# Moving two small normalisation products, one drain and one projection copy within a causal attention kernel

## The chip, the cores and the metric

The kernel runs on one core of one Trainium2 chip. The metric is device time in microseconds (us) for the whole program, from its first to its last instruction; the figure given is the median of three runs. Everything is 32-bit float. The names of the engines are those of the profile: PE for matrix products and PEld for their weight loads, ACT for ScalarE, DVE for VectorE, POOL for GpSimd, and SP for the engine whose queue here only issues transfers.

## The reference

The input `x` is 32 images of 256 channels by 32 by 32, that is 32 batches of 256 channels by 1024 positions. Group normalisation is followed by strictly causal attention of 8 heads with 32 channels each, and the result is added to `x`:

```python
g = gn(x)                                   # 32 groups of 8 channels, over channels and positions
q  = q_w  @ g + q_b                         # 256 x 1024
kv = kv_w @ g + kv_b                        # k, v: 256 x 1024 each
scores = (q^T k) / sqrt(32)                 # per head; a position sees only earlier ones
attn = softmax(scores), 0 where masked      # position 0 sees none and gets 0
return x + attn @ v
```

## The kernel before

**Visits.** A batch is worked off in N = 12 *visits*, six for each half of the heads (`g` = 0, 1). The list `visits` (L506 to L517) says which two pieces of the transposed score matrix a visit computes: one "full" piece of 512 columns by 128 keys for four heads, and one "half" piece of 256 columns. The main loop (L606 to L615) writes every engine's queue by hand, visit by visit over all 32 x 12 visits, and engines follow this order strictly. In visit `i` the loop puts down

1. `scores(i)` (L301): PE computes the two pieces into three PSUM tiles of two banks (tag `sT`, three buffers, so each visit uses all three); ACT takes three exponentials of 1024 columns each, two of the full piece (L326, into `e`) and one of the half piece (L327, into `eh`); POOL masks the diagonal (L294) where the piece has one;
2. what is filed under `at[i]`: most often one projection of the next or the same batch, 16 or 32 products into a PSUM bank and one ACT copy out of it (`project_qk`, L221, or `project_v`, L237), and issues of transfers by SP;
3. `values(i - 1)` (L338): PE multiplies the exponentials of the visit before with `v` into the bank `acc`; DVE adds the exponentials up (L354) for the softmax's denominator; at the end of a half row ACT copies `acc` to `num` (L357);
4. what is filed under `after[i]`: steps of the normalisation, folds of the sums, finishing steps.

Visits are counted below from 0 to 11 within a batch; "the fourth visit" is number 3.

**One spare bank.** [...] six hold the scores, one is `acc`, and the last has the tag `misc` with one buffer (L129, L132). Through it go, one after the other, the projection of each visit, the two products of the normalisation (`pm` in `norm_mean`, L184, and `pv` in `norm_variance`, L201) and the denominators of a whole batch (`pd` in `sum_folded`, L373). Each of these must wait until ACT has copied the one before it out of the bank. (In the first batch a few projections use `acc` instead, L159.)

**Projections.** The twelve projections of a batch are placed at visits -5 to 6 (`PROJECT`, L538), so one falls into each visit: visits 7 to 11 serve the next batch, visits 0 to 6 the present one. The last, in visit 6, is `k` of the second half of the heads.

**Normalisation** of batch b (`prepare`, L524) has eight steps filed under `after`, placed by `PREPARE` (L539) relative to the batch's first visit: DVE statistics of the two channel halves (-18, -17), the product `pm` with its ACT copy (-16, that is visit 8 two batches ahead), the deviation on DVE (-15), the product `pv` with its ACT copy (-14), the power on POOL (L209, at -12) and the two halves of the normalised `xn` on DVE (L216, both at -11, which is visit 1). The first two batches are placed separately.

**Denominators.** For each batch but the last two, POOL issues two adding transfers for each of the four half rows (`fold`, L363): partitions 64 to 127 onto 0 to 63 after visit `SUMS[n]` = 3, 7, 9, 13 and 32 to 63 onto 0 to 31 two visits later. The second waits for the landing of the first, and both stand in POOL's queue with the masks. Two more visits later SP brings the 32 rows into `folded` (`stack`, L367). In visit 18, which is visit 6 of the next batch, PE sums them (`pd`), ACT copies the result, and SP sends it through DRAM; DVE inverts it (L439), and `finish` (L453, DVE) writes the output after visits 12, 12, 13 and 14 of the next batch. SP also loads `x` two batches ahead, in visit 3 (`load`, L115), behind the output stores of visits 0 to 2.

**`shifted`** (L625) is a second, safe program under a condition that is false for these inputs; only it reads `v_bias` (L683), which is loaded at the start (L143).

Of the kernel before, what the change touches and what calls it, by code (L numbers as in the profile page):

```python
# [9 lines left out]
F32 = mybir.dt.float32  # L10
I32 = mybir.dt.int32
AF = mybir.ActivationFunctionType
# [5 lines left out]
P = 128  # L18
HD = 32
# [12 lines left out]
def tile_norm_attention_residual(  # L32
# [19 lines left out]
    nc = tc.nc  # L52
    B, C, H, W = x.shape
# [51 lines left out]
    wT = const.tile([P, NG, 3 * C], F32, name="wT")  # L105
    qk_bias = const.tile([P, 2, NG], F32, name="qk_bias")
    v_bias_col = const.tile([P, NG], F32, name="v_bias_col")
    v_bias = const.tile([P, C], F32, name="v_bias")

    def unshifted():  # L110
        live = {}
# [24 lines left out]
        def load_weights():  # L136
            for n, w in enumerate((q_w, kv_w[0:C], kv_w[C : 2 * C])):
                live["wn", n] = epool.tile([P, 4, HALFBANK], F32, tag="eh", bufs=4, name=f"wn_{n}")[:, :NG, :C]
                nc.scalar.dma_start(out=live["wn", n], in_=w.rearrange("(o p) c -> p o c", p=P))
            nc.scalar.dma_start(out=qk_bias[:, 0, :], in_=q_b.rearrange("(g p) -> p g", p=P))  # L140
            nc.scalar.dma_start(out=qk_bias[:, 1, :], in_=kv_b[0:C].rearrange("(g p) -> p g", p=P))
            nc.scalar.dma_start(out=v_bias_col, in_=kv_b[C : 2 * C].rearrange("(g p) -> p g", p=P))
            nc.scalar.dma_start(out=v_bias, in_=kv_b[C : 2 * C].rearrange("(o c) -> o c", o=1).broadcast_to([P, C]))  # L143

        def turn_weights(n):
            wn = live["wn", n]
# [151 lines left out]
            if k == 0:  # L298
                nc.gpsimd.memset(e[0:1, :, 0:1], 1.0)

        def scores(b, full, half):  # L301


            tag = "e0" if full[2] == 0 else "e"
            name = f"{b}_{full[0]}_{full[1]}_{full[2]}"
            e = epool.tile([P, 4, HALF], F32, tag=tag, bufs=4 if tag == "e0" else 3, name=f"{tag}_{name}")
            eh = epool.tile([P, 4, HALFBANK], F32, tag="eh", bufs=4, name=f"eh_{name}")
            pairs = [ps_s.tile([P, 2, HALF], F32, tag="sT", name=f"sT_{name}_{a}") for a in range(3)]
            short = pairs[2].rearrange("p bank (n q) -> p bank n q", n=2)
            first = [scores_of((b, half), short[:, j % 2, 1, :], j) for j in (2, 3)]  # L310
            for j in range(4):
                scores_of((b, full), pairs[j // 2][:, j % 2, :], j)

            for ins in first:
                ins.then_inc(bank_free, 1)
                tc.no_tile_sem_insts.add(ins.ins.name)
            live["free"] = live.get("free", 0) + len(first)
            wait = nc.tensor.wait_ge(bank_free, live["free"])
            for ins in first:
                tc.declare_no_dep(wait.ins, ins.ins, reason="the semaphore orders them")  # L320
            for j in range(2):
                lo = scores_of((b, half), short[:, j, 0, :], j)
                for ins in first:
                    tc.declare_no_dep(lo.ins, ins.ins, reason="the semaphore orders them")
            for a in range(2):
                nc.scalar.activation(e[:, 2 * a : 2 * a + 2, :], pairs[a], AF.Exp)  # L326
            exp = nc.scalar.activation(eh.rearrange("p (n bank) q -> p bank n q", n=2), short, AF.Exp)  # L327

            for ins in first:
                tc.add_to_no_dep_group(f"first_{name}", ins.ins)  # L330
                tc.add_to_no_dep_group("first", ins.ins)
            tc.declare_no_dep(exp.ins, group=f"first_{name}", reason="through the last two products")
            tc.declare_fence(exp.ins, group=f"first_{name}")
            mask(full, e)
            mask(half, eh)
            live["e", b, full], live["e", b, half] = e, eh
# [25 lines left out]

        def fold(b, n, rows):  # L363
            total = live["sum", b, *divmod(n, NH)]
            nc.gpsimd.dma_start(out=total[:rows], in_=total[rows : 2 * rows], accum_op=ALU.add)  # L365

        def stack(b, n):  # L367
# [168 lines left out]


        PROJECT = (-5, -4, -3, -2, -1, 0, 1, 2, 3, 4, 5, 6)  # L538
        PREPARE = (-18, -17, -16, -15, -14, -12, -11, -11)  # L539
        SUMS = (3, 7, 9, 13)  # L540

        FINISH = ((N + 12, N + 12, N + 13, N + 14), (N + 7, N + 7, N + 8, N + 9))
# [1 line left out]

        with tc.manual_schedule(engines={ENG.PE, ENG.Activation, ENG.DVE, ENG.Pool}):
            load_weights()
            turn_weights(0)
            for g in range(NG):
                norm_channels(0, g)
            keep_busy(2)  # L550
            norm_mean(0)
            turn_weights(1)
            norm_deviation(0)
            norm_variance(0)
            norm_rstd(0)
            turn_weights(2)
            keep_busy(4)
            for hf in range(NH):
                norm_apply(0, slice(hf * HALF, (hf + 1) * HALF))
            nc.vector.tensor_scalar_mul(qk_bias[:, 0, :], qk_bias[:, 0, :], SCALE)  # L560
            units = projections(0)
            for n, f in zip((None, None, 0, 0, 0, 0) + PROJECT[6:], units):
                if n is None:
                    f()
                else:
                    when(n, f)
            if B > 1:
                prepare(1, (None, None, 0, 1, 2, 3, 3, 3))
            for b in range(B):
                first, last, late = b * N, b == B - 1, b >= B - 2  # L570
                if b >= 1:
                    for n, f in zip(PROJECT if not last else PROJECT[:-1] + (8,), projections(b)):
                        when(first + n, f)
                if b >= 2:
                    when(max(first - 2 * N + 3, 0), lambda b=b: load(b))
                    prepare(b, [first + n for n in PREPARE])
                for n in every:
                    v = first + (N if last and n == 3 else SUMS[n])
                    if last and n == 3:
                        for i in (N - 1, N):  # L580
                            when(first + i, lambda b=b, i=i: sum_pieces(b, products[i - 1], i == N - 1, i == N), after)
                    if late:
                        when(v, lambda b=b, n=n: sums(b, *divmod(n, NH)), after)
                    else:
                        when(v, lambda b=b, n=n: fold(b, n, 2 * HD), after)
                        when(v + 2, lambda b=b, n=n: fold(b, n, HD), after)
                        when(v + 4, lambda b=b, n=n: stack(b, n))
                if not last:
                    if not late:
                        when(first + N + 6, lambda b=b: sum_folded(b), after)  # L590
                    v = first + N + (2 if late else 8)
                    when(v, lambda b=b: gather(b, every))
                    when(v + 2, lambda b=b: check_sums(b, every))
                    when(v + 2, lambda b=b: invert(b, every))
                    for n in every:
                        when(first + FINISH[late][n], lambda b=b, n=n: finish(b, n), after)
                else:
                    when(first + N - 4, lambda b=b: gather(b, every[:2]))
                    when(first + N - 3, lambda b=b: check_sums(b, every[:2]))
                    when(first + N - 3, lambda b=b: invert(b, every[:2]))  # L600
                    when(first + N, lambda b=b: check_here(2, in_range[:, ROW : ROW + 1]))
                    when(first + N, lambda b=b: invert_here(b, 2, slice(0, HALF)))
                    when(first + N, lambda b=b: finish(b, 2))
                    for n in every[:2]:
                        when(first + N, lambda b=b, n=n: finish_aside(b, n), after)
            for i in range(B * N + 1):  # L606
                if i < B * N:
                    scores(i // N, *visits[i % N])
                for f in at.pop(i, ()):
                    f()  # L610
                if i:
                    for pc in products[(i - 1) % N]:
                        values((i - 1) // N, pc, i < B * N - 1)
                for f in after.pop(i, ()):
                    f()  # L615
            assert not at and not after
            outside = end_last(B - 1)
# [7 lines left out]
    def shifted():  # L625

        with ExitStack() as inner:
# [3 lines left out]
            ps_b = inner.enter_context(tc.tile_pool(name="g_ps_b", bufs=2, space=PSUM))  # L631
            ps_c = inner.enter_context(tc.tile_pool(name="g_ps_c", bufs=2, space=PSUM))

            masked_bias = pool.tile([P, 1], F32, name="masked_bias")
            nc.gpsimd.memset(masked_bias, MASKED)

# [136 lines left out]
```

## Time and profile before

| | |
|---|---|
| median of three runs | 1902.81 us (1902.04 to 1903.99) |
| span of the profiled run | 1900.5 us |
| mean granted TensorE clock | 0.997 |
| DVE, ACT, POOL busy | 83%, 74%, 42% |
| HBM traffic over the span | 55 GB/s |
| exponential of 1024 columns (L326) | 1022 ns, 768 of them |
| addition of 1024 columns (L354) | 1428 ns, 382 of them |
| copy of a `q` or `k` projection (L233) | 701 ns, 256 of them |
| half of `xn` for one channel half (L216) | 541 ns, 128 of them |
| power on POOL (L209) | 1583 ns, 32 of them |

The page of the profile gives each engine's busy time and, in its fourth part, the chain of work that ended last: what the end of the program was waiting for, followed backwards. The trace also answers with a timeline (instructions in order of time with the idle time before each and what ended it, in brackets), a list of waits (who waited for whom: total in us, how often, longest) and the chain in order of time.

Two details are needed in reading it. PE's rows overlap: the end of a product is modelled, and the next one starts a little before it. And the program is so regular that visits can be compared by their length, taken here as the time from one visit's first score product to the next visit's in PE's timeline. The medians over batches 2 to 29, in us:

| visit | 0 | 1 | 2 | 3 | 4 | 5 | 6 | 7 | 8 | 9 | 10 | 11 |
|---|---|---|---|---|---|---|---|---|---|---|---|---|
| length | 4.65 | 4.74 | 4.22 | 5.09 | 4.66 | 4.74 | 5.67 | 4.74 | 4.84 | 5.08 | 4.75 | 4.75 |

Visits k and k + 6 do the same attention work for the two halves of the heads. Only visit 6 varies between batches, from 5.66 to 6.43 with a mean of 5.81; the other eleven keep within 0.01.

### The profile page before, as it was taken

How to read it: one execution, taken by the hardware profiler on the slowest of the kernel's cores; microseconds unless marked ns; L12 is line 12 of the kernel's file. 1: busy time of each engine (PE TensorE's matmuls, PEld its weight loads, DVE VectorE, ACT ScalarE, POOL GpSimd, SP SyncE). 2: the span in 40 equal slices, each digit the busy share in tenths (PEclk: the TensorE clock that was granted, in tenths of full speed). 3: DMA queues.
4: the chain of work that ended last, by engine and by line, in shares of the span. 5: the costliest groups of instructions: out<-in, count | busy, mean ns of one | idle time of the engine just before them, and what ended most of it. 6: DMA issues, size and time to landing. Idle time of an engine off the chain costs nothing.

```text
span 1900.5 us, 54083 instructions
## 1 busy us (share of the span) xinstructions
PE 1860.3 (98%) x23410; PEld 944.9 (50%) x23410; DVE 1569.0 (83%) x1604; ACT 1410.1 (74%) x1775; POOL 802.5 (42%) x741
## 2 busy tenths in 40 slices
PE   8999999999999999999999999999999999999996
PEld 4544555554554545554545544455545455444552
DVE  3778988888988889888889888898888898888877
ACT  5777777777777777777777777777777777777775
POOL 2443444534444435444344444354443444443413
PEclk9999999999999999999999999999999999999998
DMA  3457666666666676666666656766567666667312
GB/s 120 68 83 145 132 139 114 120 134 136 138 125 126 122 144 131 140 115 118 134 138 137 133 116 124 142 132 140 113 123 134 135 140 128 121 121 143 83 56 73
DMA packets 77660, 233.54 MB, mean 123 GB/s; under 512 B 19824, under 2 KB 20976, under 8 KB 62056
## 3 DMA queue, kind: packets, MB, share of 16 engines
q0 software_dynamic: 15360, 94.39, 36.9%
q1 hardware_dynamic: 60280, 134.72, 23.4%
q8 instruction: 185, 3.03, 0.7%
q10 hardware_dynamic: 1776, 0.92, 0.2%
q14 instruction: 59, 0.48, 0.1%
HBM read 68.54 MB, written 35.62 MB: 55 GB/s over the span
## 4 chain that ended last, share of the span: by engine, by line
PE 89%; ACT 5%; DMA 2%; issue 2%; DVE 1%; POOL 0%; ACTq 0%; POOLq 0%; SPq 0%; DVEq 0%
PE sT L279 29%; PE acc L349 24%; PE pp L171 21%; PE ppv L171 12%; ACT e L326 2%; PE pd L384 2%; ACT eh L327 1%; DMA folded<-e 1%; ACT k L233 1%; DVE e L354 0%; PE pm L171 0%; DMA wn<-in_L_conv_kv_w_dram 0%; DVE rb L472 0%; DVE rb L457 0%; DVE rb L458 0%
## 5 line engine op out<-in xcount | busy, mean ns | idle before, releaser
L326 ACT ACTIVATE e<-sT 128x1024 f32<-128x1024 f32 x768 | 744.9, 1022 | 407.4 <-PE sT L279 359.7
L354 DVE TENSOR_TENSOR e<-e,eh 128x1024 f32<-128x1024 f32 x382 | 540.1, 1428 | 278.1 <-PE acc L349 250.1
L294 POOL TENSOR_SCALAR_AFFINE_SELECT e<-e 128x512 f32<-128x512 f32 (+1 forms) x256 | 387.1, 1512 | 698.1 <-ACT e L326 673.9
L354 DVE TENSOR_TENSOR e<-e,e 128x1536 f32<-128x1536 f32 x381 | 638.4, 1676 | 25.0 <-POOL e L294 4.0
L279 PE MATMUL sT<-q,k 32*128 32x256 f32 (+3 forms) x7168 | 617.5, 460 | 0.8 <-ACT k L233 0.8
L279 PEld LDWEIGHTS sT<-q,k 32*128 32x128 f32 x7168 | 463.4, 184 | 170.5 <-ACT q L233 50.6
L171 PE MATMUL pp<-xn,wT 128*32 128x512 f32 x4096 | 492.3, 598 | 0.0
L349 PE MATMUL acc<-e,v 128*32 128x512 f32 (+2 forms) x4096 | 400.7, 486 | 0.0
L327 ACT ACTIVATE eh<-sT 128x1024 f32<-128x1024 f32 x384 | 396.6, 1033 | 0.0
L365 POOL DMA_DIRECT2D e<-e x240 | 197.4, 862 | 364.8 <-DMA e<-e 205.9
L171 PE MATMUL ppv<-wT,xn 128*32 128x256 f32 x4096 | 247.3, 382 | 0.0
L349 PEld LDWEIGHTS acc<-e,v 128*32 128x32 f32 x4096 | 132.6, 110 | 223.1 <-issue 200.7
L349 PE MATMUL acc<-eh,v 128*32 128x256 f32 x3072 | 224.4, 379 | 0.0
L171 PEld LDWEIGHTS pp<-xn,wT 128*32 128x32 f32 x4096 | 107.0, 109 | 218.3 <-issue 200.0
L349 PEld LDWEIGHTS acc<-eh,v 128*32 128x32 f32 x3072 | 98.5, 110 | 164.2 <-issue 152.6
L171 PEld LDWEIGHTS ppv<-wT,xn 128*32 128x32 f32 x4096 | 120.2, 109 | 102.0 <-issue 32.1
L294 POOL TENSOR_SCALAR_AFFINE_SELECT eh<-eh 128x512 f32<-128x512 f32 x128 | 164.0, 1281 | 1.1
L457 DVE TENSOR_TENSOR rb<-num,rb 128x512 f32<-128x512 f32 (+1 forms) x127 | 110.9, 873 | 0.1
L458 DVE SCALAR_TENSOR_TENSOR rb<-rb,v_bias_col,x 128x512 f32<-128x512 f32 (+1 forms) x127 | 96.1, 757 | 4.5
L233 ACT ACTIVATE q<-pp,qk_bias 128x512 f32<-128x512 f32 x128 | 89.8, 702 | 4.5 <-PE pp L171 4.5
L233 ACT ACTIVATE k<-pp,qk_bias 128x512 f32<-128x512 f32 x128 | 89.6, 700 | 2.2 <-PE pm L171 1.1
L357 ACT COPY num<-acc 128x512 f32<-128x512 f32 x128 | 76.4, 597 | 15.9 <-PE acc L349 15.9
(69 smaller groups left out, 499.2 us busy)
## 6 DMA issues: line engine op xcount, KB each, us to landing
e<-e POOLq DMA_DIRECT2D x120, 512.0 KB, 7.9
x<-in_x_dram SPq DMA_DIRECT2D x64, 512.0 KB
out_dram<-rb SPq DMA_DIRECT2D x127, 256.0 KB
rb<-inverses SPq DMA_DIRECT2D x126, 256.0 KB
e<-e POOLq DMA_DIRECT2D x120, 256.0 KB, 4.6
folded<-e SPq DMA_DIRECT2D x120, 256.0 KB
rows<-sums SPq DMA_DIRECT2D x31, 32.0 KB
inverses<-inv SPq DMA_DIRECT2D x31, 32.0 KB
```

Source lines behind the costliest of these rows:

```text
L171: nc.tensor.matmul(out[part], lhsT=lhsT[:, part], rhs=rhs, start=start, stop=stop, skip_group_check=True)
L233: nc.scalar.activation(live[key][:, cols], pp, AF.Identity, bias=qk_bias[:, n, g : g + 1], scale=(SCALE, 1.0)[n],)
L279: ins = nc.tensor.matmul(pair[:, cols], lhsT=live["k", b, g][rows, kb * P : (kb + 1) * P], rhs=live["q", b, g][rows, hf * HALF + of.start ...
L294: nc.gpsimd.affine_select(out=diagonal, in_=diagonal, pattern=[[0, 4], [0, n], [1, P]], compare_op=ALU.is_gt, fill=0.0, base=0, channel_mu ...
L326: nc.scalar.activation(e[:, 2 * a : 2 * a + 2, :], pairs[a], AF.Exp)
L327: exp = nc.scalar.activation(eh.rearrange("p (n bank) q -> p bank n q", n=2), short, AF.Exp)
L349: nc.tensor.matmul(acc[HD * j : HD * (j + 1), of], lhsT=live["v", b][:, kb, h * HD : (h + 1) * HD], rhs=e[:, j, cols], start=first, stop=l ...
L354: nc.vector.tensor_add(total[:, :, of], total[:, :, of], e[:, :, cols])
L357: nc.scalar.copy(num, acc)
L365: nc.gpsimd.dma_start(out=total[:rows], in_=total[rows : 2 * rows], accum_op=ALU.add)
L457: nc.vector.tensor_mul(rb, num[:, within], rb)
L458: nc.vector.scalar_tensor_tensor(rb, rb, v_bias_col[:, g : g + 1], xt[:, g, cols], ALU.add, ALU.add)
```

## The change

Four edits are made.

- The products `pm` and `pv` and what belongs to them go to the visits 3 and 4 of the batch before (-9 and -8), the power with them (-8), and the two halves of `xn` to visits 5 and 6 (-7, -6). This shortens the time between the products and their use and takes them out of visits 8 and 10.
- In a visit 6 that has something filed under `at`, that is the projection, `scores` puts it down between the exponentials: ACT takes the first exponential of the full piece, that of the half piece, then the projection's copy, and last the second exponential of the full piece. The order on PE stays as it was. The denominators' product in the same visit uses the bank that this copy frees.
- POOL gets one `drain` in each batch but the last two, ahead of the second fold of half row 1 (after visit 9).
- `v_bias` is loaded in `shifted`, where it is used, and not at the start.

```diff
-    v_bias = const.tile([P, C], F32, name="v_bias")
...
-            nc.scalar.dma_start(out=v_bias, in_=kv_b[C : 2 * C].rearrange("(o c) -> o c", o=1).broadcast_to([P, C]))
...
-        def scores(b, full, half):
+        def scores(b, full, half, between=()):
...
-            for a in range(2):
-                nc.scalar.activation(e[:, 2 * a : 2 * a + 2, :], pairs[a], AF.Exp)
-            exp = nc.scalar.activation(eh.rearrange("p (n bank) q -> p bank n q", n=2), short, AF.Exp)
+            for a in (0, 2, 1) if between else (0, 1, 2):
+                if a == 1:
+                    for f in between:
+                        f()
+                if a == 2:
+                    exp = nc.scalar.activation(eh.rearrange("p (n bank) q -> p bank n q", n=2), short, AF.Exp)
+                else:
+                    nc.scalar.activation(e[:, 2 * a : 2 * a + 2, :], pairs[a], AF.Exp)
...
             total = live["sum", b, *divmod(n, NH)]
+            if (n, rows) == (1, HD):
+                nc.gpsimd.drain()
             nc.gpsimd.dma_start(out=total[:rows], in_=total[rows : 2 * rows], accum_op=ALU.add)
...
-        PREPARE = (-18, -17, -16, -15, -14, -12, -11, -11)
+        PREPARE = (-18, -17, -9, -9, -8, -8, -7, -6)
...
-                    scores(i // N, *visits[i % N])
+                    between = at.pop(i, ()) if i % N == 6 else ()
+                    scores(i // N, *visits[i % N], between)
...
+            v_bias = pool.tile([P, C], F32, name="v_bias")
+            nc.sync.dma_start(out=v_bias, in_=kv_b[C : 2 * C].rearrange("(o c) -> o c", o=1).broadcast_to([P, C]))
```

## The prediction, made before the changed kernel was run

> **What bounds the kernel now.** I read the page first: busy times, then the chain that ended last.
>
> ```profile
> PE 1860.3 (98%) x23410; PEld 944.9 (50%) x23410; DVE 1569.0 (83%) x1604; ACT 1410.1 (74%) x1775; POOL 802.5 (42%) x741
> ...
> PE 89%; ACT 5%; DMA 2%; issue 2%; DVE 1%; POOL 0%; ACTq 0%; POOLq 0%; SPq 0%; DVEq 0%
> ```
>
> PE is busy 98% of the span and is 89% of the chain. So the order of PE's queue sets the end, and only what moves a product on PE counts. The chain leaves PE in one place per batch, at the end of visit 8 (the chain in order of time; start, length, what):
>
> ```profile
> 932.33 1.09 PE sT L279 x8
> ...
> 935.38 0.92 ACT eh L327
> 936.30 0.58 ACT k L233
> 936.88 0.04 issue
> 936.93 0.24 PE pm L171 x8
> ...
> 946.90 0.09 PE pv L171 x8
> ```
>
> PE stands before `pm` until ACT has taken three exponentials and copied the projection `k` out of the one spare bank. Visit 8 has the shortest value products (0.86 us for its twin, visit 2, in the chain; 1.29 in most visits), so PE is done before ACT. `pv` after visit 10 costs only 0.09. The list of waits says how often (us in total, times, longest):
>
> ```profile
> PEld pm L171 <- ACT k L233: 19.4, 30, 0.7
> ...
> PEld pd L384 <- ACT k L233: 15.5, 29, 1.1
> ...
> PE pm L171 <- ACT k L233: 11.4, 30, 0.4
> ```
>
> The same copy holds `pd` in visit 6. One batch's timeline, PE and then ACT:
>
> ```profile
> 1039.22 1.92 PE L171 MATMUL pp<-xn,wT 128*32 128x512 f32 x16
> 1040.97 1.05 PE L349 MATMUL acc<-e,v 128*32 128x384 f32 x16
> 1041.83 0.61 PE L349 MATMUL acc<-eh,v 128*32 128x256 f32 x8
> 1042.39 1.06 PE L384 MATMUL pd<-folded,pick_half 128*32 128x512 f32 x8
> ```
> ```profile
> 1040.73 1.03 ACT L327 ACTIVATE eh<-sT 128x1024 f32<-128x1024 f32 x1
> 1041.64 0.70 ACT L233 ACTIVATE k<-pp,qk_bias 128x512 f32<-128x512 f32 x1
> ```
>
> The projection ends at 1041.14, but its copy starts at 1041.64, behind the exponentials; it ends at 1042.34 and `pd` follows 0.05 later. Last, POOL and SP:
>
> ```profile
> 931.78 0.85 POOL L365 DMA_DIRECT2D e<-e  x1
> 937.59 1.61 POOL L365 DMA_DIRECT2D e<-e  x2 [4.95 <-DMA e<-e]
> 945.38 2.48 POOL L294 TENSOR_SCALAR_AFFINE_SELECT e<-e 128x512 f32<-128x512 f32 x1 [6.19 <-ACT e L326]
> ```
> ```profile
> 970.71 2.83 SPq L118 DMA_DIRECT2D x<-in_x_dram  x2
> 974.63 13.09 SPq L371 DMA_DIRECT2D folded<-e  x2
> ```
>
> POOL idles 4.95 us ahead of the fold that gets the drain, and 6.19 ahead of the next mask.
>
> **What the Trainium skill says.** "PSUM — Partial Sum Buffer", section "Engine vs sequencer instructions": the queues of ScalarE, VectorE and GpSimd are strictly first in, first out, and products start in program order; a drain waits for its engine to go fully idle. The trace agrees on the order (`k` waits behind `eh` though its input is ready); it has no drain. "SBUF — State Buffer", "SBUF: two separate sides": a DVE operation with two SBUF inputs and a GpSimd operation that reads SBUF exclude each other. It fits: a mask of 512 columns takes 0.71 us in visit 6 (1040.93) but 1.92 in visit 4. "TensorEngine Tiling (Array Packing)", "Key Properties": a change of tiling mode drains TensorE. A small part of a visit's length is that: in visit 6 the next scores start 1.00 after `pd`'s start, though eight products stream in 0.87 (sixteen take 1.75 from 1039.22 to 1040.97).
>
> **Part 1, `pm` and `pv` to visits 3 and 4.** Removed: visit 8 is 4.842, its twin visit 2, with the same work and no `pm`, 4.220, so 0.622 a batch go. Visit 10 against its twin 4: 4.750 against 4.657, 0.093 go. Added: in visit 3 the copy of `v` ends 4.58 after the visit's start and the value products, the longest of all (1.72), end at 5.15, so the bank is free about 0.5 before `pm`'s turn; it costs its eight tiny products, between 0.05 (seven in the first batch, unheld: 27.20 in the chain) and 0.09 (`pv` now); I take 0.07. Visit 4 is timed like visit 10, so `pv` costs 0.093 again. Sum: 0.622 - 0.07 = 0.55 a batch, times 30 batches = 16.6 us.
>
> New neighbours. `pv` needs the deviation, three DVE operations of 0.16 queued behind visit 3's additions. These end 2.2 into visit 4 before the change (from the DVE timeline, in every batch), so the deviation is ready near 2.8 and `pv`'s turn comes at 4.6. ACT's small copies (0.18 and 0.26) fall into idle time of 0.9 to 1.6 before the next visit's exponentials. The power, 1.67 in visit 0, would start some 0.4 into visit 5 when POOL has just ended visit 4's mask, and that queue's next mask starts 3.2 into the visit: hidden. The halves of `xn` (2 x 0.54 each) leave visit 1, where DVE ran up to 3.6 behind PE, for visits 5 and 6, where it is 1.2 and 0.4 behind; DVE idles 2.9 in visit 7 and 4.5 in visit 9. The first half is ready about 2 into visit 6, the projection that reads it starts 1.6 into visit 7. Cost nothing.
>
> **Part 2, the copy ahead of one exponential.** The copy starts 0.08 after its products' end (as after the first batch's wait, 16.08 to 16.16), at 1041.22, and ends at 1041.92. Then the bank is free 0.4 before the value products end, and `pd` follows them directly. Visit 6 is 5.665 in undisturbed batches; without a wait it is visit 0's 4.652 plus 0.87 = 5.52. That is 0.14 x 30 = 4.3 us.
>
> In 13 batches `pd` starts later still, by 0.02 to 0.76, in sum 4.2 us: there the copy has long ended, and the rows of `folded` are what lands last. The edit doesn't touch that, but part 1 might: SP issues the last `folded` behind the load of `x`, that behind the output store of visit 2, and DVE did `xn` (1.9) ahead of that store's operands. With it gone the load leaves up to 1.9 earlier. I count 60%, 2.5 us; bounds 0 and 4.2.
>
> Queued behind the copy: the second exponential now ends 5.10 into the visit instead of 3.13, so visit 6's masks start at 5.15. Two masks and a memset take from 1.7 (now) to 4.2 (both at the slow ends seen, 2.48 and 1.66), ending at 6.9 to 9.4. Their readers on PE come in visit 7, at about 8.9 (`e`) and 9.7 (`eh`). Hidden, with 0.3 left at the worst. ACT's copies of `num` and `pd` end at 5.6 and 6.2, the next exponential starts at 6.7.
>
> **Part 3, the drain.** The trace has none. Lower bound: 12 ns, what "VectorE: DVE Perf Modes", "The DRAIN you can't avoid", gives for boilerplate drains. Upper bound: all that POOL has before it, the issue of 0.85. I take the upper one; the 4.95 of waiting behind it hides it. A mask would come late only beyond 6 us.
>
> **Part 4, `v_bias`.** One issue of 0.51 on ACT's queue at 5.39 goes. PE waits then for another transfer (`wn`, landing at 8.65) and later for its filler products until 14.2. I take 0, at most 0.4.
>
> **One loss.** In visit 3 of batch 30, `after` holds denominators of its own ahead of `pm`, so `pm` waits for their copy (0.585 + 0.1): 0.7 us, once.
>
> **Sum:** 16.6 + 4.3 + 2.5 - 0.7 = 22.7; 1902.8 - 22.7 = 1880.1, given as 1880.
>
> **The rivals.** (a) *`pd` stays bound by `folded`.* For: 13 of 30 batches show it already, and PE arriving earlier makes it show more. Against: 17 batches start exactly 0.05 after the copy. Then only 15.9 is won: 1887; 16%. (b) *A new wait in visits 3 to 6* takes the place of the old, the deviation or `xn` coming late behind DVE's additions, half a microsecond a batch. For: DVE is 83% busy and its order is strict. Against: margins of 1.8 and 5 us. 1880 + 15 = 1895; 10%. (c) *Slower.* POOL is the new bound: visit 6's masks, starting 2 us later among DVE's two-input additions and the moved `xn`, hold the value products of visit 7, or the drain costs far more than I allow. With both masks slow and one more blocked by a DVE addition (1.5) the wait is 1.2 to 1.5 a batch: 30 x 1.3 = 39, 1880 + 39 = 1919; 8%. Against: in visit 6 no mask took over 1.6.
>
> **How the numbers follow.** The main case, 1876 (all late `folded` and the start gained) to 1884 (neither, and `pm` at 0.09 or a little more), has 64%; with a further 2% for effects that cancel. The range 1876 to 1889 takes in (a), in sum 80%. Faster by over 0.2%: main, (a) and (b), 0.90; same 0.02; slower 0.08.
>
> **What would show it.** Right: visits 8 and 10 at 4.22 and 4.66, visits 3 and 4 at about 5.15 and 4.75; `pm`'s wait on `k` gone from the list; visit 6 at 5.52 in most batches. (a) would show as `pd` waiting on `folded` in most batches, (b) as `pv` waiting on `dev` or `pp` on `xn`, (c) as `acc` waiting on POOL's `e` or `eh` in visit 7. I would be wrong if a visit that no edit touches grew.

## The result

The changed kernel takes 1875.86 us (median of four runs, 1874.11 to 1877.28) against 1902.42 for the kernel before: a ratio of 0.986, 95% interval 0.9842 to 0.9877. It is faster by 26.6 us where 22.4 had been forecast from that median (22.7 in the working), and lies 0.14 us below the forecast range, 1876 to 1889.

The page of the profile after, in the two lines that were shown of before:

```profile
PE 1850.8 (99%) x23410; PEld 950.6 (51%) x23410; DVE 1573.4 (84%) x1604; ACT 1413.7 (75%) x1775; POOL 765.5 (41%) x741
...
PE 97%; DVE 1%; DMA 0%; ACT 0%; issue 0%; ACTq 0%; DVEq 0%
```

PE is 97% of the chain now, against 89%, and ACT's 5% are gone. One batch of the chain in order of time (start, length, what), with visit 3 ending in `pm`, visit 4 in `pv`, visit 6 in `pd`, and visit 8 with its 0.86 of value products running straight into the next scores:

```profile
898.29 1.71 PE acc L353 x22
900.00 0.05 PE pm L169 x7
...
904.70 0.09 PE pv L169 x8
...
912.90 1.29 PE acc L353 x24
914.19 0.86 PE pd L390 x8
915.05 1.60 PE sT L277 x18
...
923.15 0.86 PE acc L353 x16
924.01 1.50 PE sT L277 x12
```

In the timeline of the same visit 6 (PE first, then ACT), the copy now waits only for its products and no longer stands behind an exponential, and `pd` follows the value products directly:

```profile
910.97 1.92 PE L169 MATMUL pp<-xn,wT 128*32 128x512 f32 x16
...
914.01 1.04 PE L390 MATMUL pd<-folded,pick_half 128*32 128x512 f32 x8
```
```profile
912.96 0.69 ACT L231 ACTIVATE k<-pp,qk_bias 128x512 f32<-128x512 f32 x1 [0.37 <-PE pp L169]
913.55 1.02 ACT L331 ACTIVATE e<-sT 128x1024 f32<-128x1024 f32 x1
```

The lengths of the visits, medians over batches 2 to 29 in us, measured in the same way as ahead of the prediction:

| visit | 0 | 1 | 2 | 3 | 4 | 5 | 6 | 7 | 8 | 9 | 10 | 11 |
|---|---|---|---|---|---|---|---|---|---|---|---|---|
| before | 4.65 | 4.74 | 4.22 | 5.09 | 4.66 | 4.74 | 5.67 | 4.74 | 4.84 | 5.08 | 4.75 | 4.75 |
| after | 4.65 | 4.74 | 4.22 | 5.12 | 4.75 | 4.74 | 5.51 | 4.74 | 4.22 | 5.08 | 4.66 | 4.75 |

With the start (up to the first score product), the last batches and the end (from the start of the last visit) this accounts for the whole difference of the two profiled spans, 1900.5 and 1874.0:

| where | forecast, us | found, us |
|---|---|---|
| `pm` and `pv`: visits 3, 4, 8, 10, thirty times (-0.622 - 0.093 + 0.036 + 0.091) | -16.6 | -17.6 |
| `pd`: visit 6, thirty times (-0.155) | -4.3 | -4.7 |
| visits 6 that were later still: 4.2 before in 13 batches, 2.3 after in 3 | -2.5 | -1.9 |
| batch 30, visit 3 (6.89 in place of 5.95, less the 0.036) and visit 7 | +0.7 | +0.9 |
| start, 18.61 to 19.02 | 0 | +0.4 |
| **end, 27.37 to 23.71** | **0** | **-3.7** |
| sum | -22.7 | -26.5 |

The sum is 3.8 larger than the forecast. The end makes up 3.7 of that; the misses of the other lines, -1.0, -0.4, +0.6, +0.2 and +0.4, nearly cancel, which is chance. The end was not in the forecast at all. It holds no work of the four edits: after the last visit there are the last sums, inversions and stores, and then the program's own closing, in which each engine drains. POOL's closing drain is what differs. The answers for the closing line of the program, before and after (shortest, middle and longest of three, in ns):

```profile
L769 POOLq DRAIN  x3: 38/98/9779, 1889.9 to 1900.2; - x3
L769 SPq DRAIN  x3: 7/7/7, 1895.7 to 1899.9; - x3
```
```profile
L779 POOLq DRAIN  x3: 46/98/459, 1866.9 to 1873.7; - x3
L779 SPq DRAIN  x3: 7/7/7, 1873.1 to 1873.4; - x3
```

Before, POOL's drain lasts 9.78 us, from 1889.88 to 1899.66, while SP has closed its queue at 1895.8: the program waits 3.9 us for POOL alone. In the changed kernel it lasts 0.46 and ends long before SP. The drains in the batches were seen to be this long, 6.0 to 6.7 us and not the 0.85 at most that the prediction allowed:

```profile
L370 POOLq DRAIN  x30: 6025/6167/6682, 59.7 to 1721.0; - x30
```

### The profile page after: what moved, and what is told of

Read it like the earlier page. It is cut to its first block, busy times and chain, and to the rows that moved or that the text cites. A ratio compares the mean times of both kernels' runs of the same rounds, so it can differ in the third digit from the quotient of the medians.

```text
span 1874.0 us, 54145 instructions
## 1 busy us (share of the span) xinstructions
PE 1850.8 (99%) x23410; PEld 950.6 (51%) x23410; DVE 1573.4 (84%) x1604; ACT 1413.7 (75%) x1775; POOL 765.5 (41%) x741
## 4 chain that ended last, share of the span: by engine, by line
PE 97%; DVE 1%; DMA 0%; ACT 0%; issue 0%; ACTq 0%; DVEq 0%
PE sT L277 31%; PE acc L353 26%; PE pp L169 25%; PE ppv L169 13%; PE pd L390 2%; DVE e L358 1%; DMA wn<-in_L_conv_kv_w_dram 0%; DVE rb L464 0%; DVE rb L463 0%; DVE rb L478 0%; ACT e L331 0%; PE pv L169 0%; PE busy L155 0%; ACT k L231 0%; PE pm L169 0%
## 5 line engine op out<-in xcount | busy, mean ns | idle before, releaser
L358 DVE TENSOR_TENSOR e<-e,eh 128x1024 f32<-128x1024 f32 x382 | 534.5, 1413 | 247.2 <-PE acc L353 215.1
L292 POOL TENSOR_SCALAR_AFFINE_SELECT e<-e 128x512 f32<-128x512 f32 (+1 forms) x256 | 359.4, 1404 | 678.5 <-ACT e L331 657.9
L358 DVE TENSOR_TENSOR e<-e,e 128x1536 f32<-128x1536 f32 x381 | 618.0, 1622 | 16.9 <-POOL e L292 2.6
L464 DVE SCALAR_TENSOR_TENSOR rb<-rb,v_bias_col,x 128x512 f32<-128x512 f32 (+1 forms) x127 | 114.1, 898 | 4.5
L463 DVE TENSOR_TENSOR rb<-num,rb 128x512 f32<-128x512 f32 (+1 forms) x127 | 90.4, 711 | 11.6 <-DMA rb<-inverses 11.3
L214 DVE TENSOR_SCALAR xn<-x,mean,rstd 128x512 f32<-128x512 f32 x128 | 96.7, 796 | 2.0 <-POOL rstd L207 2.0
```

The costliest lines, as they stand in the source:

```text
L214: nc.vector.tensor_scalar(live["xn", b][:, g, cols], live["x", b][:, g, cols], mean[:, g : g + 1], rstd[:, g : g + 1], ALU.subtract, ALU.mult,
L292: nc.gpsimd.affine_select(out=diagonal, in_=diagonal, pattern=[[0, 4], [0, n], [1, P]], compare_op=ALU.is_gt, fill=0.0, base=0, channel_mu ...
L358: nc.vector.tensor_add(total[:, :, of], total[:, :, of], e[:, :, cols])
L463: nc.vector.tensor_mul(rb, num[:, within], rb)
L464: nc.vector.scalar_tensor_tensor(rb, rb, v_bias_col[:, g : g + 1], xt[:, g, cols], ALU.add, ALU.add)
```

## The experiments

The theory (A): the closing drain does work that has piled up with every adding transfer (fold) issued since the last drain, and the drains in the batches take it away in time that nobody waits for. Its rivals: (B) the end is shorter by chance or through another edit; (C) the drains cost something in the visits. For the later visits 6 the question was whether they became rarer because moving `xn` lets the load of `x` leave earlier, as the prediction had it, or through the drain or the copy.

**Without the drains.**

```diff
 # the changed kernel
-            if (n, rows) == (1, HD):
-                nc.gpsimd.drain()
```

> The changed kernel without the drains. Theory A (the program's own last drain on POOL does work that piles up with every fold not yet drained; 9.78 us before, 0.46 after): the last drain takes about 9.8 us again, the time from the last visit's start to the end goes from 23.7 back to 27.4, every visit stays as in the changed kernel, the total is 1875.9 + 3.7 = 1879.6. Rival B (the shorter end comes from something else in the change or from chance): the end stays at 23.7 and the total at 1875.9. Rival C (the drains of 6 us within the batches cost something in the visits too): the visits get shorter without them, total below 1879.

Measured: 1878.1 us (1877.13 to 1880.18), ratio to before 0.9866 (0.9848 to 0.9883). The end is 27.24 again and the closing drain what it was before:

```profile
L777 POOLq DRAIN  x3: 34/98/9779, 1866.0 to 1876.3; - x3
L777 SPq DRAIN  x3: 7/7/7, 1872.2 to 1876.0; - x3
```

SP is done at 1872.2 and POOL at 1875.8. B falls. The total rises by 2.2 and not 3.7. In the profiles the span grows by 2.6: the end takes 3.5 more and the time up to the first score product 1.3 more, while no visit 6 is late here (5.51 in all thirty), which is 2.3 less. The medians of all visits are the same to 0.01, so there C finds nothing; whether the drains make some visits 6 late is taken up below.

**The drains alone.**

```diff
 # the kernel before
+            if (n, rows) == (1, HD):
+                nc.gpsimd.drain()
```

> The kernel before with the drains alone. Theory A: last drain about 0.5 us, end 23.7 in place of 27.4, all visits as before: 1902.4 - 3.7 = 1898.7. Rival B: 1902.4, end 27.4. Rival C: visits 9 and 10 longer, total above 1898.7.

Measured: 1899.5 (1895.05 to 1903.01), ratio 0.9983 (0.9973 to 0.9992), 3.1 us less than before. The end is 23.77, the closing drain 0.46, and visits 9 and 10 are 5.08 and 4.75 as before. A holds in both directions. Eleven batches have a late visit 6, with 1.9 us in sum.

```profile
L771 POOLq DRAIN  x3: 46/98/459, 1887.7 to 1894.5; - x3
```

**The moved normalisation alone.**

```diff
 # the kernel before
-        PREPARE = (-18, -17, -16, -15, -14, -12, -11, -11)
+        PREPARE = (-18, -17, -9, -9, -8, -8, -7, -6)
```

> The kernel before with the moved normalisation alone. Visits 8 and 10 at 4.22 and 4.66, 3 and 4 at 5.12 and 4.75: 30 x 0.59 = 17.6 us, less 0.9 in batch 30. If the moved halves of xn (x loaded earlier) are what brings the rows of folded in time, visit 6 is 5.67 with about 3 late batches in place of 13: about 2 us more, 1883.8. If the late rows came in time for another reason (the drain, or the copy), visit 6 stays late in about 13 batches: 1885.7. The end stays at 27.4 in both.

Measured: 1881.57 (1881.31 to 1883.07), ratio 0.9885 (0.9868 to 0.9902). Visits 3, 4, 8 and 10 are 5.12, 4.75, 4.22 and 4.66, the end 27.36, and visit 6 is 5.66 or 5.67 in all thirty batches: the late ones are gone altogether, and the total is below both branches.

**The copy alone.**

```diff
 # the kernel before
-            for a in range(2):
-                nc.scalar.activation(e[:, 2 * a : 2 * a + 2, :], pairs[a], AF.Exp)
-            exp = nc.scalar.activation(eh.rearrange("p (n bank) q -> p bank n q", n=2), short, AF.Exp)
+            for a in (0, 2, 1) if between else (0, 1, 2):
+                if a == 1:
+                    for f in between:
+                        f()
...
```

> The kernel before with the projection's copy ahead of one exponential alone. Visit 6 at 5.51 in the batches where folded lands in time. If folded's landing isn't moved by this edit, about 13 batches stay at their late lengths (5.69 to 6.43) and 17 x 0.155 = 2.6 us are won: 1899.8. If the edit also brings folded in time, 30 x 0.155 + 4.2 = 8.9 us: 1893.5. The end stays at 27.4.

Measured: 1898.01 (1895.01 to 1899.47), ratio 0.9966 (0.9954 to 0.9979). Visit 6 is 5.51 in 14 batches and later in 16, up to 7.20, with `pd` now waiting for the rows themselves:

```profile
PE pd L390 <- DMA folded<-e: 2.9, 5, 1.5
```

By the visits the edit alone wins 1.9 us: the first branch, with part of the gain lost because PE, arriving earlier, finds the rows still missing. The timed gain is larger, 4.6; in the profile another 2.2 lie ahead of the first visit, where the edit changes nothing (see the end of this document). I go by the visits.

**Only the two halves of `xn`,** to find which part of the normalisation it is.

```diff
 # the kernel before
-        PREPARE = (-18, -17, -16, -15, -14, -12, -11, -11)
+        PREPARE = (-18, -17, -16, -15, -14, -12, -7, -6)
```

> The kernel before with only the two halves of xn moved, to visits 5 and 6. If they hold back the load of x and with it folded: the load of x is issued about 3.1 and not 5.4 into visit 3, visit 6 is 5.67 in nearly all batches, 4 us won: 1898.5. If not: late in about 13 batches, 1902.5. All other visits as before.

Measured: 1897.84 (one run). The kernel before, run once beside this run and the three that follow, took 1905.57, more than its median elsewhere, so these four are read from their visits. The load of `x` leaves 3.59 into visit 3 (before 5.41), visit 6 takes 5.66 or 5.67 in all thirty batches, and every other visit and the end are as before; the visits give 4.2 us. So the copies on DVE had held the store, the store the load, and the load the rows of `folded`, all in SP's one queue. How often a visit 6 is late differs between kernels that share the place of `xn`, and each has one profile: 6 to 16 batches with `xn` in its old place (2.9 us in 6 batches in the run with `pm` in visit 9, 4.2 us in 13 before), 0 to 3 with it moved. The two ranges don't meet, but the size of this gain is known only roughly. The lines of SP in one batch of the changed kernel show the load behind the last store:

```profile
893.84 4.11 SPq L467 DMA_DIRECT2D out_dram<-rb  x2
898.01 0.93 SPq L117 DMA_DIRECT2D x<-in_x_dram  x2
```

In the changed kernel's own three late batches (9, 20 and 27) the load was issued 5.7, 6.7 and 5.7 into visit 3, otherwise 3.15 in most and never over 4.7: the same mechanism, set off there by a late last output step on DVE. For these steps the changed kernel's list of waits names inverses that land late (`DVE rb L463 <- DMA rb<-inverses`, 11.3 us in 11 waits). Why they land late in those batches is not shown. A drain is not needed for it: in the runs below with their first drain in batch 15 and in the last batch, batch 9 is late all the same (6.34 and 6.51). That the drains, which push the second folds back by about 0.6 us, add to it is possible and not shown.

**`pm` one visit later, all else in place.**

```diff
 # the kernel before
-        PREPARE = (-18, -17, -16, -15, -14, -12, -11, -11)
+        PREPARE = (-18, -17, -15, -15, -14, -12, -11, -11)
```

> The kernel before with pm moved by one visit, from 8 to 9 whose value products are the longest, and all else in its place. If what counts is how long the value products ahead of pm are: visit 8 at 4.22, visit 9 at 5.08 + 0.04, 30 x 0.58 = 17.5 us in all, 1885; visit 6 late in about 13 batches as before, end 27.4. If it is the place of the whole chain that counts (pv, the power, xn moved too): visit 9 longer by up to 0.6 and nothing won.

Measured: 1883.46 (one run). Visit 8 is 4.22 and visit 9 5.11, 0.03 longer: 0.59 a batch, by moving one product by one visit. `pv`, in visit 10 as before, costs its 0.09 there as in visit 4. What counts is how long PE's value products run before `pm`, not where the chain as a whole stands.

**What a drain costs.** If its work piles up, one drain in the middle must be long. The next two kernels change only the condition of the drain.

```diff
 # the changed kernel
-            if (n, rows) == (1, HD):
+            if (b, n, rows) == (15, 0, HD):
```

> The changed kernel with one drain only, in batch 15 ahead of the second fold of half row 0, where no adding transfer is on its way. From 9.78 us after 240 folds and 0.46 after 5, a drain would take 0.26 + 0.0397 for each fold since the last one. Theory A (it is this piled-up work): the drain in batch 15 comes after 121 folds and takes about 5.1 us, the last one after 119 takes about 5.0; the end stays short (about 23.8), because 5.0 us fit beside the end of the other queues. Rival D (a drain waits only for transfers on their way, and the 9.78 have another source): under 0.5 us in batch 15 and 9.78 at the end.

Measured: 1884.78 (one run), slower than the changed kernel, and neither branch fits. The line of the drain in the batch comes first, then the closing line:

```profile
L370 POOLq DRAIN  x1: 11971/11971/11971, 909.5 to 909.5; - x1
```
```profile
L779 POOLq DRAIN  x3: 46/98/9779, 1872.1 to 1882.4; - x3
```

The drain comes after 121 folds and takes 12.0 us, 2.0 of them a mask that still runs as it begins. The last one, after 119, takes 9.78, as much as after 240. So D falls, and A stands with a higher price, which can't go on growing up to 240 folds. The masks queued behind the drain came late, and visit 7 of batch 15 was 10.86 long in place of 4.74: here a drain's own time reached PE.

```diff
 # the changed kernel
-            if (n, rows) == (1, HD):
+            if (n, rows) == (0, HD):
```

> The changed kernel with the drain of each batch ahead of the second fold of half row 0, where the first fold has landed, and not of half row 1, where it is on its way. If the 6.0 us of the drain were the wait for that transfer: 0.26 + 8 x 0.04 = 0.6 us here, the visits as in the changed kernel and few or no late visits 6. If a drain takes 6 us by itself: 6 us here too, masks of visit 6 starting at 7.8 and not 5.2 into the visit, visit 7 longer by 1 to 2 us a batch. The last drain at about 0.5 in both.

Measured: 1872.32 (one run), every visit as in the changed kernel, no visit 6 late, end 23.50:

```profile
L370 POOLq DRAIN  x30: 2726/2732/3658, 49.8 to 1707.7; - x30
```
```profile
L779 POOLq DRAIN  x3: 46/98/622, 1863.2 to 1870.0; - x3
```

The drains take 2.73 in place of 6.17 where no fold is on its way: most of the 6 us was the wait for the transfer. Of the 2.73, 2.0 are a mask that still runs as the drain begins. The closing drain takes 0.62 after seven folds, 0.46 after five: 0.08 a fold, twice my estimate.

To see the whole curve, drains at growing distances:

```diff
 # the changed kernel
-            if (n, rows) == (1, HD):
+            if (n, rows) == (0, HD) and b in (0, 1, 3, 7, 15, 29):
```

> The changed kernel with drains ahead of the second fold of half row 0 in batches 0, 1, 3, 7, 15 and 29 alone, that is 1, 8, 16, 32, 64 and 112 folds after the one before, and 7 folds ahead of the last. Last drains so far: 0.04 after no fold, 0.46 after 5, 0.62 after 7, 9.78 after 119 and after 240. Theory E (0.082 us for each fold since the last drain, up to a most of 9.78): with the 2.1 us of mask that stands before it (2.73 with 8 folds), 3.4, 4.7, 7.3 and 11.3 after 16, 32, 64 and 112, and 0.62 at the end. Rival F (a step: short after few folds, all of the 9.78 from some number on): about 2.7 or 3.4 up to a point, then 11.9, with nothing between.

Measured: 1881.13 (one run; 1899.41 for the kernel before beside it). The drains after 16, 32, 64 and 112 folds, by the line's answer in a window around each, and under the last of them the mask that runs as it begins:

```profile
L370 POOLq DRAIN  x1: 3386/3386/3386, 220.0 to 220.0; - x1
```
```profile
L370 POOLq DRAIN  x1: 4692/4692/4692, 448.8 to 448.8; - x1
```
```profile
L370 POOLq DRAIN  x1: 7309/7309/7309, 907.0 to 907.0; - x1
```
```profile
L370 POOLq DRAIN  x1: 11226/11226/11226, 1710.6 to 1710.6; - x1
```
```profile
1710.93 1.66 POOL L292 TENSOR_SCALAR_AFFINE_SELECT eh<-eh 128x512 f32<-128x512 f32 x1
```

The drains took 3.39, 4.69, 7.31 and 11.23 against 3.4, 4.7, 7.3 and 11.3 expected: (11.23 - 3.39) / 96 = 0.082 us a fold, a straight line, and 0.62 at the close. F falls. The mask is done 2.0 us after the drain's start, so 9.22 of the 11.23 come after it. Drains this long are not free: in batch 29 the masks behind the last one came so late that visits 7 and 8 took 8.90 and 5.72, and the batches after the drains of 4.69 and 7.31 had a late visit 6 (6.16 and 6.91).

**One drain where POOL has nothing to do,** and the loss in batch 30 mended.

```diff
 # the changed kernel
-            if (n, rows) == (1, HD):
-                nc.gpsimd.drain()
...
-                    v = first + (N if last and n == 3 else SUMS[n])
+                    v = first + (N if last and n == 3 else 5 if late and not last and n == 0 else SUMS[n])
...
                 else:
+                    when(first + 1, lambda: nc.gpsimd.drain(), after)
```

> The changed kernel with one drain in all, in the last batch after visit 1, where POOL has nothing to do for over 9 us and all folds have landed, and with the denominators of batch 30's first half row two visits later (visit 5), so that pm doesn't wait for their copy in visit 3. Theory A: that drain takes about 9.8 us, hidden, the last one under 0.5, the end is 23.7; no fold is held by a drain, so no visit 6 is late (2.3 us against the changed kernel's profile); batch 30's visit 3 is 5.12 and not 6.89, its visit 5 about 0.9 longer: 0.9 us. Total about 1873. Rival: a drain of that length there holds the masks of the last batch, whose visits 4 to 6 get longer by 1 to 5 us: above 1875.

Measured: 1871.95 (1871.13 to 1874.62), ratio to before 0.9841 (0.9827 to 0.9854): the fastest of the kernels with more than one run, some 4 us under the changed kernel's median. The drain, the mask that it finds running, and the closing line:

```profile
L602 POOLq DRAIN  x1: 10929/10929/10929, 1805.9 to 1805.9; - x1
```
```profile
1805.91 1.10 POOL L292 TENSOR_SCALAR_AFFINE_SELECT e<-e 128x1024 f32<-128x1024 f32 x1 [2.02 <-ACT e L331]
```
```profile
L778 POOLq DRAIN  x3: 34/41/98, 1863.4 to 1870.2; - x3
```

The one drain takes 10.9 us, 1.1 of them that mask, in a gap of 14.7 between two masks, and no visit of the last batch is longer for it. The closing drain takes 0.04 although the masks of the last batch lie between the two drains, so POOL's masks alone do not bring the cost. The end is 23.71, as with thirty drains. Batch 30 has 5.12 in visit 3 and 5.74 in visit 5, 0.8 less in all. One visit 6 (batch 9, 6.51) was late, 1.3 less than in the changed kernel's profile. The rest of the difference of the two profiles, 1.5 of 3.5, lies ahead of the first score product, where the kernels are the same.

## Why the prediction was wrong

**Parts 1 and 2 held, step by step.** Twins among the visits gave the gain of moving `pm` (0.622 removed, found 0.62) and `pv` (0.093 and 0.093, found 0.09 and 0.09). The one estimate, 0.07 for `pm` in visit 3, was 0.036. For `pd`, the 0.14 from streaming time alone was 0.155: after the change the chain has 0.86 for its eight products, not 0.87. That none of the hidden work would show, deviation, power, `xn` and visit 6's masks, came out as said: visits 5 and 7 are unchanged, and rival (b)'s half microsecond and rival (c)'s late value products didn't come. The load of `x` left 2.3 us earlier and took away 1.9 of the 4.2 us of later visits 6 in the two profiles, 45% where 60% had been allowed; with `xn` moved alone they are gone altogether. Rival (a) was visible as a risk in the copy's own run only, where the load is not moved. The loss in batch 30 was 0.9 for 0.7.

**Part 3 failed.** "I take the upper one; the 4.95 of waiting behind it hides it" looked for the cost of the drain where it stands and asked only what it might delay. The sum then had no term for the drain and none for the end of the program. Two things were wrong in it. Its price, at most 0.85, took POOL's queue for all that a drain waits for; in fact it waited for the transfer on its way as well, 6.2 us in the median. That is only about 0.6 longer than the second fold would have waited anyway, so the conclusion that it is hidden survived by luck. And it took the edit's effect to lie within the batches. The term missing from the sum is -3.7 us at the end of the program: the closing drain after 240 undrained folds (9.78 us) was the last thing the program waited for, and the thirty drains reduced it to 0.46. The run without drains and the run with drains alone show this term by itself, -3.5 and -3.6 in the length of the end. With it, the forecast of 1880.1 would have been 1876.4.

"The trace has none" was a misreading. The trace of before has drains, the 9.78 us of POOL among them, under the last line of the program (L769). They are not in the chain of waits, which I had followed only through the batches: the last operation of DVE ends at 1892.3 and the span at 1900.5, and I never asked what fills these 8.2 us. The same line shows what the lower bound of 12 ns is worth: the closing drains of ACT, PE, DVE and SP take 7 to 17 ns, POOL's 9779. The statement of the Trainium skill ("PSUM — Partial Sum Buffer", "Engine vs sequencer instructions"), that a drain waits for its engine to go fully idle, was read as a danger only. That a drain can take 9.78 us when the last fold landed 103 us before it began, only the trace shows.

The range had little room for a term left out. Its lower edge, 1876, was given for the case "all late `folded` and the start gained"; those two add 1.7 and 0.4 to the gain, which makes 1878.0, so about 2 us were left, against the 3.7 of the end.

**What stays open.** "Piled-up work" is a name for a duration that grows with the number of folds; what POOL does in that time, and why it is 0.082 us a fold, no run shows. Nor does one show why 240 folds cost no more than 119. A ceiling does not fit exactly: once the running mask is done, the drain after 121 folds has 9.97 us left and the one after 240 has 9.80, about two folds less. It would fit if the share of the first 121 had gone on the way, without a drain, since 240 - 121 = 119; that is a guess from these numbers. Part 4 can't be told apart from chance: the first score product comes between 16.4 and 20.3 us in the profiles of all these kernels, with `v_bias` loaded at the start (16.4 to 18.9) or not (17.2 to 20.3).

## What to carry to other kernels

Before predicting, account for the span from its first to its last microsecond, the closing included: what each queue still does after the last operation, and which of them ends last. Where a shared bank is released by a copy at the end of a strict queue, put the next user behind the longest independent work and the copy ahead of whatever needn't come first; repeated structures in the trace (here twin visits) price such moves to a hundredth of a microsecond. What POOL's closing drain had to do could be done here in any gap that is long enough: one drain of 10.9 us in a gap of 14.7 did as well as thirty. Where the gap was too short, a drain of 12.0 us made a visit 6.1 longer.

## What the runs showed that had not been expected

- POOL's drain takes 0.082 us for each adding transfer issued on its queue since the last drain, even long after these have landed (112 folds: 11.23 us less 2.0 of mask), 9.78 at the close after 119 and after 240, and 0.04 after none.
- With a transfer on its way it ends 0.2 to 0.4 us after that lands: it takes 6.0 to 6.7 us right behind a fold, against 2.73 with none under way.
- The halves of `xn`, put into visits with masks, take 796 ns on average instead of 541: about 0.9 us for most of those that overlap a mask, 0.54 for those that overlap nothing on POOL. The lock between DVE and GpSimd that the Trainium skill describes ("SBUF — State Buffer", "SBUF: two separate sides") is a possible reason; that these operations, with one tensor as input, come under it was not tried. None of it reached PE.
- The time up to the first score product spreads by almost 4 us over the profiles (16.4 to 20.3). Each kernel has one profile, so whether this is the spread between runs of one kernel isn't shown; differences of one or two us are therefore read from the visits and not from the totals.
